# One transfer per unit for the time steps of a state-space scan

## The chip, the cores and the metric

The kernel runs on one core of a Trainium2 chip. The metric is the device time of one execution in microseconds (us). Of three timed executions of the kernel before the change the median is 6779.58 us (6778.02 to 6794.15). A separate execution was recorded by the hardware profiler; the profile below is of that one.

## The reference, cut to what matters

Four layers work on a batch of four images of 32 x 32 positions (1024 tokens) with 256 channels: a convolution with a state-space scan (layer 0), a bottleneck convolution (layer 1), masked attention with a mixture of experts (layer 2), and a second state-space scan with a mixture of experts (layer 3). The change touches the two scans alone. Both have 512 inner channels; the first has N = 64 states for each channel, the second N = 16. In layer 0, with `xt`, `dtt`, `Bt` and `Ct` of one token:

```python
dt = softplus(dt_raw @ w_dt + dt_bias)        # [batch, token, 512]
A = -exp(A_log)                               # [512, N]
def step(h, inp):
    xt, dtt, Bt, Ct = inp
    dA = exp(dtt[:, :, None] * A)
    h = dA * h + (dtt * xt)[:, :, None] * Bt[:, None, :]
    y = einsum('bdn,bn->bd', h, Ct)
    return (h, y)
```

Layer 3 does the same with its own `dt`, `A`, `B`, `C` and N = 16. What matters below: `dt` has one value for each channel and token, and every state of a channel needs that same value, multiplied by its own entry of `A`.

## The kernel before

**Units of a scan.** A scan of one image is cut into units. One unit fills the 128 partitions with the (channel, state) pairs of G = 128 / N channels: partition g * N + s holds state s of the unit's channel g. So G is 2 in layer 0 and 8 in layer 3. The free dimension holds the 1024 tokens. Scan (0, b) is that of layer 0 for image b and has 256 units; scan (3, b) is that of layer 3 and has 64. They run in the order `SCANS` of line 31: (0,0), (0,1), (3,0), (0,2), (3,1), (0,3), (3,2), (3,3); 1280 units in all, of which 1024 have G = 2 and 256 have G = 8.

**What one unit does** (`scans`, line 351). The steps of unit k are:

- `load` (line 416): G DMAs, issued by SyncE (SP in the profile). Each reads one row of 1024 floats (4 KB) of `dt` from DRAM and writes it to the N partitions of its channel, into its part of the tile `dA` (128 x 1024 floats, 512 KB). The tile has five buffers.
- `decay` (line 431): ScalarE turns the tile in place into exp(A * dt); A comes as a scale for each partition.
- `first` (line 441): two TensorE matmuls spread dt * x over the states into the PSUM tile `ps_rep`.
- in the loop (line 497): VectorE multiplies `ps_rep` by the tile of B (`rows`).
- line 503: VectorE runs the recurrence with `tensor_tensor_scan` from `dA` and `ps_rep` into `h`; line 504: GpSimd multiplies `h` by the tile of C.
- `pair` (line 456): for every two units TensorE sums over the states into `ps_y`; at the end of a group ScalarE copies the result to `yo`, and SP stores it.

**Order.** The order of every engine's instructions is fixed when the program is built. At step k the loop first calls `load(k + 4)`, then `first(k + 1)`, then `decay(k + 2)`; the VectorE work of unit k follows. As `dA` has five buffers, the load of unit k + 4 waits until the scan of unit k - 1 has read the last tenant of its buffer. SP issues all loads and stores of the kernel from one queue, in order: when it waits for a buffer, everything behind it waits too. Each DMA also waits for the one issued eight before it, since eight semaphores are used in turn.

**What runs between the units.** The other layers are generators (`front`, `middle`, `last`, line 33) that yield a piece of work at a time. `run` (line 548) puts up to two pieces between the steps of the scan, by estimated costs of instructions (`Metered`, line 92) kept in a clock for each engine; the estimates do not count DMAs issued by SP. So TensorE, ScalarE, VectorE and GpSimd alternate between scan units and pieces of other layers, and SP between loads of `dA` and the other layers' loads and stores, such as expert weights (`we`, lines 1452 and 1454), the scan results read back (`y_back`, line 782) and the stores of `dt` and its split product (lines 614 and 629). Before the first scan, `load_vectors` (line 191), `weight` (line 227), `rows` (line 221) and the `prepare` functions load small vectors and matrices; the vectors of `VEC_PACKS` (line 51) come with one DMA for each name, of 1 to 36 rows of 512 bytes, and `w2s` (line 859) with one of 4 rows of 9 pieces.

All compute instructions issued in the interleaved part carry line 124 in the profile, that of the wrapper that meters them. The loads of `dA` carry line 425.

Of the kernel before, what the change touches and what calls it, by code (L numbers as in the profile page):

```python
# [18 lines left out]
L = 1024  # L19
# [113 lines left out]
class Hybrid:  # L133
# [217 lines left out]
    def scans(self, mp, psum):  # L351
# [7 lines left out]
        nc = self.nc  # L359
        units = []  # L360
        for scan in SCANS:
            G = P // self.states[scan[0]]
# [53 lines left out]
        def load(k):  # L416
            if k >= len(units):
                return
            scan, d, c, i, j = units[k]
            n = self.states[scan[0]]  # L420
            G = P // n
            a = mp.tile([P, L], F32, tag="dA", name="dA", bufs=5)
            for g in range(G):
                r = 64 * c + 32 * j + G * i + g
                nc.sync.dma_start(  # L425
                    a[g * n : (g + 1) * n, :],
                    self.mem["dt", *scan, d][r : r + 1, :].to_broadcast([n, L]),
                )
            state[k] = a

        def decay(k):
# [53 lines left out]
        for k in range(4):  # L485
            load(k)
# [3 lines left out]
        for k in range(len(units) + 4):  # L490
            waits = chunks_ahead(k)
            load(k + 4)
            if not waits:
                first(k + 1)
            decay(k + 2)
            if k < len(units):
                a, inp = state.pop(k)
                B, Cm = rows[units[k][0]]
                nc.vector.tensor_tensor(inp, inp, B, ALU.mult)
            yield  # L500
            if k < len(units):
                h = mp.tile([P, L], F32, tag="h", name="h", bufs=5)
                nc.vector.tensor_tensor_scan(h, a, inp, 0.0, ALU.mult, ALU.add)
                nc.gpsimd.tensor_tensor(h, h, Cm, ALU.mult)
                state[k] = h
            if k % 2 == 1 and 2 <= k < len(units) + 2:
                pair(k - 2)
            if waits:
                chunks_ahead(k, True)
                first(k + 1)  # L510
            yield
# [1332 lines left out]
```

## Time and profile before

| what | value |
|---|---|
| timed executions | 6779.58 us median of 3 (6778.02 to 6794.15) |
| the profiled execution's own time | 6786.48 us |
| its span, first to last instruction | 6784.8 us |
| busy: TensorE, VectorE, GpSimd, ScalarE | 79%, 77%, 54%, 51% of the span |
| granted TensorE clock | 0.827 of full speed |
| DMA traffic | 937.44 MB, mean 138 GB/s |
| hardware DMA queue | 391696 packets, 930.53 MB, 52.1% of 16 engines' span |
| first and last scan instruction start | 207.4 us and 6343.7 us |
| SP waiting for VectorE's `h` before a load of `dA` | 2405.8 us in 871 waits |
| ScalarE waiting for a load of `dA` | 990.5 us in 366 waits |

The span counts from the first to the last instruction of the profiled execution; its own time lies 1.7 us above it. Busy shares are means over stages with different limits, so they do not tell what bounds a stage. An engine's wait is idle time of that engine before an instruction, put down to whatever released it last; idle time of an engine that does not bound a stage costs nothing. A DMA packet is one piece that one of the core's 16 DMA engines moves; the share of the queue is the time that packets took, over all 16. The table by stretches of time, used below, gives the busy time of each engine in a stretch, then the granted TensorE clock, the mean busy share of the 16 DMA engines and what they moved.

### The profile page before, as it was taken

What the parts mean: (1) busy time and instruction counts of PE and PEld (TensorE: products, weight loads), DVE (VectorE), ACT (ScalarE), POOL (GpSimd) and SP (SyncE); (2) the same over time, 40 slices, a digit from 0 to 9 for tenths busy, and PEclk for the clock granted to TensorE, in tenths of its full rate; (3) what the DMA queues carried; (4) which work ended last, traced back from release to release, by engine and by line L of the source; (5) the groups of instructions that cost most, each with busy time, mean ns of one, the idle gap of its engine ahead of it and who ended that gap; (6) DMA issues with size and microseconds to landing.
All of it is one profiled execution on the core that took longest, in us unless ns stands there. A gap on an engine that the chain in (4) does not pass through costs nothing. (4 is left out here: it accounts for less than half of the span.)

```text
span 6784.8 us, 65796 instructions
## 1 busy us (share of the span) xinstructions
PE 5361.8 (79%) x20236; PEld 2166.3 (32%) x20320; DVE 5227.3 (77%) x4486; ACT 3447.1 (51%) x4112; POOL 3649.0 (54%) x1801
## 2 busy tenths in 40 slices
PE   6558778679798568979689679898698688967979
PEld 3002213122252022234145232253254222514556
DVE  8778998978798997789889987898899871247411
ACT  2426666445477334557558445476386344245411
POOL 0876786755457665555856655556756551054200
PEclk8559778589798578979789789898699788977989
DMA  2556665754365765446656755456666750146221
GB/s 73 147 144 160 179 171 155 193 133 124 102 164 158 185 162 143 116 117 178 180 148 170 184 149 132 107 140 176 177 167 171 167 133 14 50 130 151 79 62 35
DMA packets 394235, 937.44 MB, mean 138 GB/s; under 512 B 83220, under 2 KB 165728, under 8 KB 392224
## 3 DMA queue, kind: packets, MB, share of 16 engines
q1 hardware_dynamic: 391696, 930.53, 52.1%
q8 instruction: 172, 2.82, 0.2%
q0 software_dynamic: 2128, 2.13, 0.2%
q14 instruction: 239, 1.96, 0.1%
HBM read 842.59 MB, written 93.95 MB: 138 GB/s over the span
## 5 line engine op out<-in xcount | busy, mean ns | idle before, releaser
L124 POOL TENSOR_TENSOR h<-h,rows 128x1024 f32<-128x1024 f32 x1280 | 3031.3, 2371 | 1999.9 <-DVE h L124 1649.9
L124 DVE TENSOR_TENSOR_SCAN h<-dA,ps_rep 128x1024 f32<-128x1024 f32 x1280 | 2925.2, 2285 | 234.0 <-issue 106.0
L124 DVE TENSOR_TENSOR ps_rep<-ps_rep,rows 128x1024 f32<-128x1024 f32 x1280 | 1552.8, 1213 | 287.8 <-PE ps_rep L124 287.3
L124 ACT ACTIVATE dA<-dA,A_L_conv_A_log 128x1024 f32<-128x1024 f32 x1024 | 1154.2, 1145 | 727.6 <-DMA dA<-dt 636.5
L124 PE MATMUL ps_rep<-S,spread_L_conv_A_log 96*128 96x512 bf16 x2048 | 766.7, 465 | 740.7 <-DVE h L124 709.1
L124 PE MATMUL ps_y<-h,collect_L_conv_A_log 128*32 128x512 f32 x4096 | 804.1, 762 | 96.0 <-POOL h L124 94.6
L124 PE MATMUL ps_h<-xTm,we 128*128 128x512 f32 x1536 | 719.4, 608 | 3.4 <-ACT h_m L124 1.8
L124 PE MATMUL ps_e<-we,h_m 128*128 128x256 f32 x3072 | 703.2, 382 | 10.9 <-ACT h_m L124 10.4
L124 ACT ACT_TABLE_LOAD x495 | 635.1, 1283 | 76.2 <-PE ps_h L124 44.4
L124 PEld LDWEIGHTS <-spread_L_conv_A_log 96*128 96x128 bf16 x2048 | 161.6, 103 | 1520.5 <-DVE h L124 1209.6
L124 PEld LDWEIGHTS ps_e<-we,h_m 128*128 128x128 f32 x3072 | 583.3, 191 | 157.2 <-issue 45.4
L124 DVE SCALAR_TENSOR_TENSOR tb<-ps_e,cw,tb 128x256 f32<-128x256 f32 x512 | 220.7, 474 | 415.5 <-PE ps_e L124 415.5
L124 ACT ACTIVATE h_m<-ps_h,cols 128x512 f32<-128x512 f32 x384 | 260.4, 686 | 473.8 <-PE ps_h L124 471.0
L124 ACT ACTIVATE dA<-dA,A_L_attn_A_log 128x1024 f32<-128x1024 f32 x256 | 293.5, 1148 | 390.3 <-DMA dA<-dt 354.0
L124 ACT ACTIVATE p<-ps_sc 128x512 f32<-128x512 f32 x432 | 234.4, 594 | 450.6 <-PE ps_sc L124 295.5
L124 PEld LDWEIGHTS ps_h<-xTm,we 128*128 128x128 f32 x1536 | 292.9, 194 | 341.8 <-issue 295.2
L124 PE MATMUL ps_at<-p,v 128*32 128x512 f32 x1024 | 357.6, 616 | 45.8 <-ACT p L124 35.1
L124 PE MATMUL ps_rep<-S,spread_L_attn_A_log 96*128 96x512 bf16 x512 | 185.4, 451 | 205.8 <-DVE h L124 184.3
L124 PE MATMUL ps_sc<-qT,kT 32*128 32x512 f32 x864 | 251.7, 654 | 42.1 <-ACTq L1248 24.5
L124 PE MATMUL ps_at<-p,ones 128*32 128x512 f32 x1024 | 275.1, 616 | 0.0
L124 PEld LDWEIGHTS ps_y<-h,collect_L_conv_A_log 128*32 128x32 f32 x4096 | 107.9, 120 | 495.9 <-POOL h L124 248.3
L124 PE MATMUL ps_cv<-pad,diag 128*128 128x512 f32 x576 | 260.4, 594 | 0.0
(311 smaller groups left out, 5012.4 us busy)
## 6 DMA issues: line engine op xcount, KB each, us to landing
dA<-dt SPq DMA_DIRECT2D x2048, 256.0 KB
dA<-dt SPq DMA_DIRECT2D x2048, 64.0 KB
we<-in_L_ffn_W_dram SPq DMA_DIRECT2D x64, 512.0 KB
parts<-parts SPq DMA_DIRECT2D x64, 384.0 KB
S<-parts SPq DMA_DIRECT2D x96, 256.0 KB
dt<-sp_r SPq DMA_DIRECT2D x64, 256.0 KB
y<-yo SPq DMA_DIRECT2D x128, 128.0 KB
y_back<-y SPq DMA_DIRECT2D x64, 256.0 KB
```

Of the source, the lines that this page charges most:

```text
L124: return got(*args, **kw)
```

## The change

Instead of one DMA for each channel of a unit, `load` issues one DMA for the unit. Its source is a view of G rows of `dt` with a repeated dimension in between: G rows, each taken n times (step 0), each of 1024 floats. Its destination is the whole tile of 128 partitions. The bytes moved into the tile are the same, 512 KB; the pieces of 4 KB are the same 128.

```diff
             a = mp.tile([P, L], F32, tag="dA", name="dA", bufs=5)
-            for g in range(G):
-                r = 64 * c + 32 * j + G * i + g
-                nc.sync.dma_start(
-                    a[g * n : (g + 1) * n, :],
-                    self.mem["dt", *scan, d][r : r + 1, :].to_broadcast([n, L]),
-                )
+            r = 64 * c + 32 * j + G * i
+            nc.sync.dma_start(
+                a,
+                self.mem["dt", *scan, d][r : r + G, :].unsqueeze(1).to_broadcast([G, n, L]),
+            )
             state[k] = a
```

In the built program the source of such a load has the dimensions 2 x 64 x 1024 (layer 0) or 8 x 16 x 1024 (layer 3), the destination 128 x 1 x 1024. Before, source and destination were 64 x 1024 or 16 x 1024 both. SP issues 1280 loads of `dA` in place of 4096 (2048 with N = 64 and 2048 with N = 16). The order of the instructions on TensorE, VectorE, ScalarE and GpSimd is unchanged, and so is the place of each unit's load among SP's other DMAs.

## The prediction

> **What bounds the kernel now.** I read the page's table of groups first, then the table by stretches of time, cut where the scans change, then SP's issues and the waits, and at last the DMA view of the first 26 us, where transfers of few rows stand. The chain of work that ended last is no help here: its engine shares add up to some 8% of the span and its long pieces lie in the tail after 6353 us.
>
> From the page:
>
> ```profile
> span 6784.8 us, 65796 instructions
> ...
> L124 DVE TENSOR_TENSOR_SCAN h<-dA,ps_rep 128x1024 f32<-128x1024 f32 x1280 | 2925.2, 2285 | 234.0 <-issue 106.0
> L124 DVE TENSOR_TENSOR ps_rep<-ps_rep,rows 128x1024 f32<-128x1024 f32 x1280 | 1552.8, 1213 | 287.8 <-PE ps_rep L124 287.3
> ```
>
> One unit costs VectorE 2.285 + 1.213 = 3.50 us, and the 1280 units 4478 of its 5227.3 busy us. Now all engines in the four long stretches, one for each scan of layer 0 (256 units each; the same view kept to `dA` counts 256 or 257 scan instructions in each):
>
> ```profile
> core 0: us, PE busy (x) PEld busy (x) DVE busy (x) ACT busy (x) POOL busy (x), PEclk, DMA share, GB/s
> 207.40:1277.50 1070.10, 767.51 (x2251) 198.08 (x2250) 946.15 (x633) 587.74 (x739) 811.56 (x435) 0.72 0.62 164
> 1277.50:2435.00 1157.50, 887.14 (x3519) 304.28 (x3541) 999.77 (x769) 582.22 (x689) 692.73 (x326) 0.80 0.56 148
> ...
> 2739.50:3874.10 1134.60, 946.01 (x3744) 405.97 (x3749) 1008.12 (x813) 707.54 (x769) 683.55 (x320) 0.86 0.59 156
> ...
> 4179.20:5314.70 1135.50, 946.26 (x3744) 406.43 (x3749) 1007.82 (x814) 707.68 (x769) 683.24 (x320) 0.86 0.59 156
> ```
>
> VectorE is busy 3961.9 of their 4497.7 us (88%); it bounds them. A unit takes 4497.7 / 1024 = 4.39 us. The 16 DMA engines are busy 56 to 62%, so they are no bound, but with less than a factor of two to spare. That spare is what this change has to be held against.
>
> SP's issues of the loads, from the view of tile `dA` (shortest, median and longest ns), and what VectorE waits for, over the whole span:
>
> ```profile
> L425 SPq DMA_DIRECT2D dA<-dt x4096: 302/444/5038, 197.2 to 6333.3; - x196
> ```
>
> ```profile
> DVE h L124 <- DMA dA<-dt: 51.1, 135, 7.7
> ```
>
> The loads cost VectorE itself only 51.1 us. ScalarE's 990.5 us of waiting for them is slack of an engine busy half the time.
>
> **What decides: over how many DMA engines one transfer is spread.** The start of the program has DMAs of few rows. The DMA view of 0 to 14 us and of 14 to 26 us (GB/s in 40 slices; packets):
>
> ```profile
> GB/s 0 0 0 0 0 82 143 29 149 266 360 377 392 366 363 386 421 410 407 291 113 21 0 0 6 4 3 1 1 3 1 1 1 1 3 4 3 12 6 6
> DMA packets 1480, 1.62 MB, mean 116 GB/s; under 512 B 104, under 2 KB 1224, under 8 KB 1480
> ```
>
> ```profile
> DMA packets 2473, 1.82 MB, mean 152 GB/s; under 512 B 508, under 2 KB 2472, under 8 KB 2472
> ```
>
> No data packet of the first window is under 512 B, so the 104 small ones are something else: one for each engine that a transfer uses. Test it: the transfers there have 128 rows (two), 36 (one), 8 (one), 4 (eight), 2 (five) and 1 (ten). If each takes the largest number up to 16 that divides its rows, that gives 2 x 16 + 12 + 8 + 8 x 4 + 5 x 2 + 10 = 104, exactly; 16 for each would be 432. In the second window a matrix of 32-byte rows gives 256 small data packets, leaving 252. The transfers with 16, 32, 64, 128 or 8 rows give 248; `w2s` (4 rows of 9 pieces each) must give the other 4. Its 36 pieces went over 4 engines, not 12: the outermost dimension decides.
>
> The new load's source has outermost dimension 2 (8 in layer 3), its destination 128. No transfer of before has two sides that differ, so the trace does not show which counts. Bounds: 2 engines (the source's) and 16 (the destination's). I take 2: each engine needs a whole share of both sides, and `w2s` is the nearest row, as its pieces were not used to spread it wider.
>
> [...]
>
> **The price of a piece.** A load of a layer 0 unit is 128 pieces of 4096 B, on two engines 64 each. Lower end: the best slice above moved 421 GB/s over 16 engines, 26.3 GB/s each, so 4096 B take 155.7 ns. Upper end: in the stretch from 207 us, 164 GB/s at 0.62 busy is 164 / (16 x 0.62) = 16.5 GB/s for a busy engine, 248 ns. There most packets come from sixteen engines reading the same 4 KB row at once; with two engines on two different rows that crowd is gone. I take 155.7 ns: 64 x 0.1557 = 9.96 us for a unit, against 4.39 us now. [...]
>
> **The sum, against the profiled span.**
>
> - Outside the four stretches: 6784.8 - 4497.7 = 2287 us, left as it is (layer 3's part below).
> - Loads of 1024 units: 65,536 pieces x 155.7 ns = 10,204 us, end to end on the same two engines.
> - Other traffic of those stretches on these two: 164 x 1070.1 + 148 x 1157.5 + 156 x 1134.6 + 156 x 1135.5 us = 701 MB, less 1024 x 0.524 = 537 MB of `dA`, leaves 164 MB, 10.25 MB for each engine: 390 us at 26.3 GB/s, 621 at 16.5. I take 500.
> - Gaps in which the two engines run empty. Four loads stand ahead of use, 40 us of queue, so SP's issue, ScalarE's exp (1.15 us) and the scan (2.29 us) lie beneath it. But another layer's load now queues behind up to four of ours; where an engine needs it at once, the scan stops, the queue drains, and it must start again: exp 1.15, scan 2.29, issue 0.44 and about 1 us until bytes move (in the GB/s line above the first slice with bytes begins at 1.75 us, and SP issued that DMA at 0.80), some 5 us. Between none and 300 places (a good third of SP's roughly 800 other DMAs) this is 0 to 1500 us. I take 350, some 70 places, as expert weights and `S` are asked for long ahead.
>
> Sum: 2287 + 10,204 + 500 + 350 = 13,341 us of span, with 1.7 us around it 13,343. The median of the timed runs is 7 us (0.1%) below the profiled one, which is nothing here: 13,340.
>
> **What is taken away counts little.** SP issues 1280 loads, not 4096. A new issue is not shown: between 0.302 us (the shortest now) and 0.588 us (the median of the stores of `yo`, L479); either is nothing beside 10 us. The wait removed is covered by the transfer that is now late: ScalarE waits for `dA`, VectorE for ScalarE, and behind VectorE's scan stand its pieces of other layers, then GpSimd and TensorE, and at last SP's next load, which needs the buffer.
>
> **Layer 3's 256 units** go over 8 engines: 16 pieces each, 2.5 us (4.0 at 248 ns), under the 4.76 us that a unit takes in 2435.0 to 2739.5 us. Cost 0 to +50 us; a gain is bounded by VectorE's idle time in the three plain stretches, 57.5 + 58.2 + 69.3 = 185 us. I take zero: VectorE waited 13.1 us for `dA` in the first of them.
>
> **Rivals.**
>
> - **Sixteen engines after all** (not slower): the destination's 128 partitions set the spread. Then a load takes at most 2 us, SP saves half or more of its issues, and what can go is VectorE's 51.1 us and a little of its idle time: 6,745 us, between 6,650 and 6,790. For it: the same bytes, pieces and partitions. Against it: `w2s`. The point from which this decides is 128 x 0.1557 us / engines + 0.4 us of other traffic < 4.39 us, that is 5 engines or more.
> - **Two engines at the crowded price** of 248 ns: 65,536 x 0.248 = 16,253; with 2287 + 621 + 350 it is 19,510 us. For it: it is the mean now. Against it: the cause of the crowd goes.
> - **One engine**, if the two sides cannot be matched: 20,407 + 2287 + 850, about 23,500 us. Only single-row transfers did this.
>
> **Chances and range.** Two engines near the full rate: 0.82. Two engines, crowded: 0.09. Sixteen or another number from five up: 0.07. One engine: 0.02. The forecast's own range goes from 12,800 (390 us of other traffic, no gaps, a little less outside) to 15,000 (all gaps, or a piece of 170 ns with part of them); it holds nearly all of the first case, and leaves out the others, 0.18 together. About 0.3% is what a measurement of this kernel can tell from no change. Faster by more than that 0.04, within it 0.03, slower 0.93.
>
> **What would show it.** The four layer 0 stretches take about 2.7 ms each; ScalarE's idle time before `dA` goes to several ms, released by the load of `dA`; the DMA share in these stretches falls to about 2 of 16 engines plus the rest, 0.15 to 0.2, and GB/s to 55 to 70; VectorE's busy time in all stays at 5227 us; SP shows 1280 issues; small packets fall by 61,440, as a unit's loads end on 2 or 8 engines in place of 2 x 16 or 8 x 16. Layer 3's stretches stay near 305 us. It would be wrong if the DMA share rose or the layer 0 stretches stayed near 1100 us.

## The result, and the profile after

| | before | after |
|---|---|---|
| timed executions | 6778.80 us median of 4 (6777.09 to 6794.15) | 13278.42 us median of 4 (13268.95 to 13293.59) |
| ratio, 95% interval | 1 | 1.958 [1.9545, 1.9616] |
| the profiled execution's own time, its span | 6786.48, 6784.8 us | 13293.59, 13291.9 us |
| layer 0's four stretches together | 4497.7 us | 10,914.2 us |
| layer 3's four stretches together | 1642.1 us | 1725.3 us |
| rest of the span | 645.0 us | 652.4 us |

The kernel takes nearly twice as long. Of the 6507 us that were added to the span, 6417 lie in layer 0's stretches, 83 in layer 3's and 7 elsewhere. Layer 3's last stretch ends with the last unit's work on VectorE, 3.5 us after the last scan starts. From the page of the kernel after, the span, all DMA packets, and the groups of the scan and of the exp before it (busy us, mean ns; then idle us before it and what ended most of that):

```profile
span 13291.9 us, 60144 instructions
...
DMA packets 332752, 936.84 MB, mean 70 GB/s; under 512 B 21780, under 2 KB 104288, under 8 KB 330784
...
L124 DVE TENSOR_TENSOR_SCAN h<-dA,ps_rep 128x1024 f32<-128x1024 f32 x1280 | 2924.8, 2285 | 3440.5 <-ACT dA L124 3270.8
...
L124 ACT ACTIVATE dA<-dA,A_L_conv_A_log 128x1024 f32<-128x1024 f32 x1024 | 1175.1, 1148 | 6635.0 <-DMA dA<-dt 6507.1
```

The work itself is the same: a scan still takes 2285 ns. What is new is the idle time before it, 3440.5 us in place of 234.0, put down to ScalarE's exp, which in turn waited for the load. The small packets fell from 83,220 to 21,780; before, the line of the DMA packets was

```profile
DMA packets 394235, 937.44 MB, mean 138 GB/s; under 512 B 83220, under 2 KB 165728, under 8 KB 392224
```

Now the stretches, as in the table before (layer 0, layer 0, layer 3, layer 0, layer 3, layer 0):

```profile
core 0: us, PE busy (x) PEld busy (x) DVE busy (x) ACT busy (x) POOL busy (x), PEclk, DMA share, GB/s
215.10:2920.20 2705.10, 889.89 (x2250) 232.75 (x2250) 923.91 (x633) 593.73 (x736) 801.22 (x435) 0.58 0.17 64
2920.20:5642.40 2722.20, 1087.96 (x3541) 349.55 (x3541) 991.17 (x769) 587.37 (x689) 685.56 (x326) 0.63 0.17 64
5642.40:5981.30 338.90, 250.82 (x1069) 89.14 (x1069) 248.85 (x195) 135.62 (x178) 168.88 (x79) 0.82 0.53 128
5981.30:8724.00 2742.70, 1220.98 (x3762) 489.05 (x3760) 1000.80 (x813) 711.39 (x767) 677.76 (x320) 0.66 0.18 65
8724.00:9059.70 335.70, 253.07 (x1067) 90.17 (x1067) 247.49 (x195) 135.02 (x177) 168.79 (x79) 0.82 0.52 130
9059.70:11803.90 2744.20, 1227.18 (x3762) 493.43 (x3762) 1002.19 (x814) 712.11 (x769) 677.83 (x320) 0.65 0.18 65
```

No engine is busy for half of a layer 0 stretch, and the DMA engines together are busy for 17 to 18%. Nothing looks loaded, because a mean over 16 engines hides two that hardly rest: 0.17 x 16 is 2.7 engines' worth, two of it for `dA`. In the packet records of the first stretch exactly two pieces of 4 KB are under way for 2440 of its 2705 us. The timeline of VectorE in a plain part of the second stretch (start us, us, then the instruction, and in brackets the idle time before it) shows the beat:

```profile
3377.39 2.29 DVE L124 TENSOR_TENSOR_SCAN h<-dA,ps_rep 128x1024 f32<-128x1024 f32 x1 [12.39 <-ACT dA L124]
3379.60 1.21 DVE L124 TENSOR_TENSOR ps_rep<-ps_rep,rows 128x1024 f32<-128x1024 f32 x1
3387.49 2.29 DVE L124 TENSOR_TENSOR_SCAN h<-dA,ps_rep 128x1024 f32<-128x1024 f32 x1 [6.69 <-ACT dA L124]
3389.70 1.21 DVE L124 TENSOR_TENSOR ps_rep<-ps_rep,rows 128x1024 f32<-128x1024 f32 x1
3397.58 2.29 DVE L124 TENSOR_TENSOR_SCAN h<-dA,ps_rep 128x1024 f32<-128x1024 f32 x1 [6.67 <-ACT dA L124]
```

A unit every 10.1 us: 3.4 us of work and 6.7 us of waiting. SP's queue shows the same beat from the other side. SP's timeline at the first units (start us, us of the run of issues):

```profile
197.22 33.35 SPq L424 DMA_DIRECT2D dA<-dt  x5
230.68 9.81 SPq L628 DMA_DIRECT2D parts<-parts  x1
240.58 4.17 SPq L613 DMA_DIRECT2D dt<-sp_r  x1
244.84 17.50 SPq L424 DMA_DIRECT2D dA<-dt  x3
```

Two loads are issued at once (0.6 and 0.5 us), the third issue holds SP for 12.3 us, and from then on each takes 9.8 to 9.9 us, with no buffer missing. We read this as full queues behind SP, in which room comes free only as the two engines move pieces. The store of `parts`, which has nothing to do with `dA`, waits in the same way. In a plain part (3362 to 3403 us) SP's issues follow one another every 9.94 us, which is 64 pieces at 155 ns.

### The profile page after: what moved, and what is told of

It reads as the page before. It is cut to its first block, busy times and chain, and to the rows that moved or that the text cites. A ratio compares the mean times of both kernels' runs of the same rounds, so it can differ in the third digit from the quotient of the medians.

```text
span 13291.9 us, 60144 instructions
## 1 busy us (share of the span) xinstructions
PE 6276.6 (47%) x20320; PEld 2421.3 (18%) x20320; DVE 5186.0 (39%) x4486; ACT 3471.3 (26%) x4112; POOL 3617.0 (27%) x1801
## 2 busy tenths in 40 slices
DMA packets 332752, 936.84 MB, mean 70 GB/s; under 512 B 21780, under 2 KB 104288, under 8 KB 330784
## 5 line engine op out<-in xcount | busy, mean ns | idle before, releaser
L124 DVE TENSOR_TENSOR_SCAN h<-dA,ps_rep 128x1024 f32<-128x1024 f32 x1280 | 2924.8, 2285 | 3440.5 <-ACT dA L124 3270.8
L124 PE MATMUL ps_rep<-S,spread_L_conv_A_log 96*128 96x512 bf16 x2048 | 874.7, 522 | 3553.1 <-DVE h L124 3503.3
L124 PE MATMUL ps_h<-xTm,we 128*128 128x512 f32 x1536 | 910.8, 740 | 766.5 <-ACT h_m L124 578.7
L124 PE MATMUL ps_e<-we,h_m 128*128 128x256 f32 x3072 | 828.2, 429 | 384.3 <-ACT h_m L124 384.1
L124 PEld LDWEIGHTS ps_e<-we,h_m 128*128 128x128 f32 x3072 | 659.4, 218 | 591.1 <-ACT h_m L124 446.9
L124 PE MATMUL ps_at<-p,v 128*32 128x512 f32 x1024 | 455.6, 806 | 495.2 <-ACT p L124 491.1
L124 PEld LDWEIGHTS ps_h<-xTm,we 128*128 128x128 f32 x1536 | 346.7, 235 | 1225.8 <-ACT h_m L124 634.8
L124 PE MATMUL ps_cv<-pad,diag 128*128 128x512 f32 x576 | 338.4, 740 | 159.1 <-ACT diag L124 159.1
L124 POOL TENSOR_TENSOR sp_l<-sp_l,sp_e 128x512 f32<-128x512 f32 x64 | 81.0, 1265 | 1066.5 <-ACT parts L124 768.9
L124 PE MATMUL ps_at<-p,ones 128*32 128x512 f32 x1024 | 369.1, 809 | 0.0
L124 PE MATMUL ps_sc<-qT,kT 32*128 32x512 f32 x864 | 314.8, 808 | 59.2 <-ACTq L1247 59.2
```

Of the source, the lines that this page charges most:

```text
L124: return got(*args, **kw)
```

## The experiments

The theory: a transfer is spread over as many engines as divide the outermost dimensions of both its sides, so layer 0's loads run on 2 engines, and the rate of those two sets the time. The rivals: the form with a repeated dimension is itself slow; or the price of a piece, not the number of engines, makes the loss. Each layer's part, the number of engines, the price of a piece and the number of transfers are taken apart below. Where stretches are given, they are cut at the first scan instruction of each scan, as before. Prices of a piece are means over the packet records of 4 KB in the stretch named.

**Each layer alone (e2, e3).** The changed load for one layer, the loop over channels for the other:

```diff
+            if n == 64:        # e2; e3 has n == 16
                 r = 64 * c + 32 * j + G * i
                 nc.sync.dma_start(a, ...unsqueeze(1).to_broadcast([G, n, L]))
+            else:
+                for g in range(G):
...
```

> The change in layer 0 alone; layer 3 has its eight transfers for each unit again. Engine theory: all of the lost time belongs to layer 0, so 13,180 to 13,280 us (at most the 90 us that the layer 3 stretches and the rest grew by comes back). If layer 3 carried a real part, the time would fall by several hundred us.

Measured: 13,236.53 us (13,236.20 to 13,236.85), ratio 1.9523 [1.9488, 1.9559]. All but a little of the loss is layer 0's, as expected.

> The change in layer 3 alone, on eight engines: 16 pieces, 2.5 us a unit; layer 0 has its two transfers again. Engine theory: within 6,730 to 6,840 us of time, as 2.5 to 4.0 us lies under the 4.76 us that such a unit takes before. Issue theory, if the form and not the engines held SP for 9 us: 256 x (9.2 - 4.8) = 1,130 us more, about 7,900 us.

Measured: 6855.54 us (6849.60 to 6864.34), ratio 1.0115 [1.0099, 1.0131]: 76 us slower, above what was expected. Layer 3's first two stretches take 328 us in place of 305, with 8 of 16 engines used: the same loads in the kernel after had exactly eight pieces of 4 KB under way for 194 of the 339 us of layer 3's first stretch (16 of 305 before). The first of them before, then two of e3:

```profile
2435.00:2739.50 304.50, 238.70 (x1068) 86.64 (x1080) 247.01 (x195) 133.98 (x177) 169.85 (x79) 0.87 0.59 147
```

```profile
2424.50:2752.50 328.00, 243.07 (x1068) 88.93 (x1080) 247.01 (x195) 135.11 (x178) 168.88 (x79) 0.83 0.57 137
3888.60:4216.50 327.90, 245.65 (x1068) 90.03 (x1080) 246.94 (x195) 135.13 (x178) 168.85 (x79) 0.83 0.56 137
```

A share of 0.57 again hides which engines it is. A 4 KB packet took 261 ns in the first of these stretches, so the 8192 pieces of its 64 loads keep each of 8 engines busy for 8192 x 0.261 / 8 = 267 us; all other packets, taken as spread evenly over 16 engines, add 52 us: 320 of 328 us. By this estimate these 8 engines are full.

**Sixteen engines with one transfer (e1).** The same one transfer for a unit, with the repeat outermost. Partition s * G + g then holds state s of channel g; the tables that depend on this order (A, `spread`, `collect`, the tiles of B and C) are built in it; the tiles of B and C come with 16 transfers in place of 80. All kernels below in this order (e6, e8, e9, e10) share that.

```diff
                 a,
-                self.mem["dt", *scan, d][r : r + G, :].unsqueeze(1).to_broadcast([G, n, L]),
+                self.mem["dt", *scan, d][r : r + G, :].unsqueeze(0).to_broadcast([n, G, L]),
```

> One load per unit as in the change, but with the partitions in the order (state, channel), so that the source's outermost dimension is the repeat: 64 x 2 x 1024 in layer 0, 16 x 8 x 1024 in layer 3. The tables of A, the spreading and collecting matrices and the rows of B and C are permuted to fit; the result is the same. Engine theory (the slower time comes from two engines moving 64 pieces each): 16 engines with 8 pieces each, a layer 0 unit back at 4.3 to 4.5 us, 6,650 to 6,850 us in all, SP's issues mostly under 1 us. Rival, issue theory (the issue of a source with a repeated inner dimension itself holds SP for about 9 us, as the median of 9.16 us in the changed kernel reads at first sight): still one issue of such a form per unit, so about 13,300 us. Rival, lateness (one large transfer lands later than two halves, five buffers are too few): between the two, well above 7,000 us.

Measured: **6640.68 us** (6639.17 to 6652.76), ratio 0.980 [0.9787, 0.9814]. It is 2% faster than the kernel before. So one transfer with a repeated dimension is not slow in itself; the place of the repeat decides. Its first stretches (layer 0, layer 0, layer 3):

```profile
203.90:1256.30 1052.40, 771.77 (x2252) 197.13 (x2250) 955.24 (x633) 585.33 (x738) 812.95 (x435) 0.71 0.52 167
1256.30:2396.00 1139.70, 873.50 (x3519) 300.28 (x3541) 996.06 (x770) 581.83 (x690) 694.80 (x326) 0.81 0.46 150
2396.00:2686.40 290.40, 234.69 (x1067) 85.62 (x1080) 246.15 (x195) 132.37 (x177) 169.88 (x79) 0.89 0.61 154
```

Against before, the DMA share of the first stretch fell from 0.62 to 0.52 with as many bytes, the layer 0 stretches together from 4497.7 to 4434.9 us, and layer 3's from 1642.1 to 1561.4. That is more than the rival of sixteen engines had allowed; the runs from e7 on look for the reason.

**Four and eight engines (e4, e5).** `dt` of layer 0 is stored two or four times, so that the source has 4 x 32 x 1024 or 8 x 16 x 1024 dimensions (the extra stores are 8 or 25 MB). Layer 3's load is the changed one.

```diff
+            q = 2 if n == 64 else 1        # e5: 4
+            nc.sync.dma_start(
+                a,
+                self.mem["dt", *scan, d][r : r + G].rearrange("g q t -> (g q) t")
+                .unsqueeze(1).to_broadcast([G * q, n // q, L]),
+            )
```

> The change, with each row of layer 0's dt stored twice in DRAM, so that a unit's source is 4 x 32 x 1024; still one load per unit with the same 128 pieces. Engine theory: four engines, 32 pieces of 155 ns = 4.97 us, with the other traffic and gaps of about 0.7 us 5.5 to 5.8 us a unit: 1024 x 5.7 + 2,350 = about 8,150 us (7,800 to 8,500). Issue theory: still about 13,300 us.

> The change, with each row of layer 0's dt stored four times in DRAM, so that a layer 0 source is 8 x 16 x 1024 as in layer 3: eight engines, 16 pieces each, 2.5 us a unit. By the criterion of the prediction (nothing lost from five engines up): at most the 6,856 us of the run with layer 3 alone changed. By what layer 3 showed on eight engines (0.3 us a unit more, although 2.5 us lies under the unit's time): 6,856 + 1024 x 0.3 = about 7,160 us.

Measured: four engines 8257.25 us (8253.11 to 8261.39), ratio 1.2179 [1.2157, 1.2201], as expected; eight engines 7220.99 us (7198.08 to 7236.84), ratio 1.0644 [1.0623, 1.0664], which is nearest to the second of the two sums: "nothing lost from five engines up" is wrong.

| engines of a layer 0 load | kernel | ns of a 4 KB packet, layer 0 | layer 0's stretches, us | time, us |
|---|---|---|---|---|
| 2 | after | 163 to 170 | 10,914 | 13,278 |
| 4 | e4 | 164 to 174 | 5895 | 8257 |
| 8 | e5 | 231 to 240 | 4848 | 7221 |
| 16 | e1 | 197 to 200 | 4435 | 6641 |

From 2 to 4 engines the stretches shrink by nearly half, as they must if the rate of the engines used sets the time. At eight the price of a piece jumps. In the second stretch of e5 (1204.7 us) 32,768 pieces at 240 ns on 8 engines are 984 us, the other packets, taken as spread evenly, 150 us on each engine: 1134 of 1204.7 us, 94% full. The extra stores are not the reason: their pieces have 2 KB, and layer 0's second to fourth stretches hold as many 2 KB packets as before, yet take 47 to 75 us more than before. With four or eight engines the form with one DMA costs little to issue. SP's issues and ScalarE's waits in the view of tile `dA`, first of e4:

```profile
L425 SPq DMA_DIRECT2D dA<-dt x1280: 500/574/9282, 200.5 to 7792.9; - x183
...
  DMA dA<-dt: 2786.8, 724
```

then of e5:

```profile
L425 SPq DMA_DIRECT2D dA<-dt x1280: 567/575/4664, 196.8 to 6774.1; - x183
...
  DMA dA<-dt: 1685.8, 531
```

The median issue is 574 and 575 ns, against 9164 with two engines.

**Different rows at the same time (e7).** The kernel before, but each transfer reads n different rows of `dt` in place of one row n times (always the same 128 rows). The units so get the `dt` of wrong channels; number, size and place of the pieces are unchanged.

```diff
-                r = 64 * c + 32 * j + G * i + g
+                r = 64 * g if n == 64 else 16 * g
...
-                    self.mem["dt", *scan, d][r : r + 1, :].to_broadcast([n, L]),
+                    self.mem["dt", *scan, d][r : r + n, :],
```

> The kernel before, each of its transfers reading 64 (or 16) different rows of dt where it read one row 64 (or 16) times; dt is so taken from wrong channels, and the output is not the reference's. Bytes, pieces, engines, issues and waits are unchanged. If the long pieces of the kernel before (mean 244 ns) come from sixteen engines reading one row at once: pieces near 160 ns, the DMA share in the layer 0 stretches from 0.56 to 0.62 down to about 0.4. The time would then tell what the crowd costs: nothing (6,780 us) if the loads are hidden, 50 to 100 us less if late loads are part of VectorE's idle time.

Measured: 6776.06 us (6767.66 to 6781.93), ratio 0.9996 [0.9987, 1.0005]. The first stretch, beside 0.62 and 164 GB/s before:

```profile
204.80:1271.20 1066.40, 765.81 (x2251) 197.21 (x2250) 942.47 (x633) 587.58 (x739) 811.85 (x435) 0.72 0.61 165
```

In layer 0's stretches a 4 KB packet takes 243 to 251 ns, against 247 to 249 before. That many engines read the same row does not make layer 0's price. In layer 3's stretches, all but the third, it does have a part: 222 to 225 ns in place of 257 to 265, but all of layer 3's stretches gain only 6 us by it.

**Two transfers for a unit, cut two ways (e6, e8).** Both in the order of e1. e6 cuts a unit into two halves of 64 neighbouring partitions, e8 into two halves of 512 columns over all 128 partitions:

```diff
+            for g in range(2):                                   # e6
+                nc.sync.dma_start(
+                    a[64 * g : 64 * g + 64, :],
+                    ...[r : r + G, :].unsqueeze(0).to_broadcast([n // 2, G, L]),
+                )
...
+            for g in range(2):                                   # e8
+                cols = slice(512 * g, 512 * g + 512)
+                nc.sync.dma_start(
+                    a[:, cols],
+                    ...[r : r + G, cols].unsqueeze(0).to_broadcast([n, G, 512]),
+                )
```

> The state-major order with two transfers for each unit again, one for each half of the partitions, each over 16 engines with 4 pieces. Same order, same rows read by each engine; only issues and semaphores per unit go from one to two. Theory A (the 140 us that the state-major kernel gained over the kernel before come mainly from VectorE's scan and ScalarE's exp waiting for one DMA semaphore in place of two, 0.06 us a unit: units of 3.54 us in place of 3.60): the 3.60 us come back, about 6,700 to 6,740 us. Theory B (the gain is from how the engines share the rows, mean 210 ns in place of 244 ns for a piece of 4 KB): the gain stays, 6,630 to 6,660 us.

> The state-major order with two transfers for each unit again, but cut along the tokens: each writes all 128 partitions, 512 of the 1024 columns, over 16 engines with 8 pieces of 2 KB. Issues and semaphores are as with the halves of the partitions; only the partitions that one transfer reaches differ. Semaphore theory alone (what the halves lost against one transfer, 209 us, is the second wait): about 6,850 us, as with the halves. [...]

Measured: halves 6849.63 us (6828.87 to 6861.12), ratio 1.0105 [1.0088, 1.0122], which neither theory had; columns 6663.92 us (6660.40 to 6668.09), ratio 0.9828 [0.9815, 0.9842], 186 us below the 6,850 of the semaphore theory: the second wait alone is not what the halves lost. But the two are not a clean pair in layer 3: with halves, the source there is 8 x 8 x 1024, and the number of small packets, 53,524 against 57,620 for the columns, is smaller by 512 x 8, as it must be if each of these 512 halves ran on 8 engines. A layer 3 stretch of the halves, then of the columns:

```profile
2416.80:2749.40 332.60, 245.14 (x1070) 89.56 (x1082) 247.29 (x196) 134.72 (x178) 168.63 (x79) 0.83 0.56 135
```

```profile
2406.60:2700.80 294.20, 240.26 (x1068) 88.20 (x1080) 246.54 (x196) 131.96 (x177) 169.50 (x79) 0.87 0.56 152
```

The halves' 332.6 us look like e3's 328.0, which also had 8 engines. The next run keeps halves for layer 0 alone.

**Halves in layer 0, whole transfers in layer 3 (e10).**

```diff
+            cuts = 2 if n == 64 else 1
+            m = P // cuts
+            for g in range(cuts):
+                nc.sync.dma_start(
+                    a[m * g : m * g + m, :],
+                    ...[r : r + G, :].unsqueeze(0).to_broadcast([n // cuts, G, L]),
+                )
```

> State-major order, layer 0's units by two transfers of 64 neighbouring partitions each (32 x 2 x 1024, 16 engines), layer 3's by one transfer (16 x 8 x 1024, 16 engines). In the earlier run with halves in both layers, a half of a unit of layer 3 had a source of 8 x 8 x 1024, and so only 8 engines. Theory A, those 8 engines made layer 3's loss: layer 3's stretches as with whole transfers, 1,561 us, layer 0's as with halves, 4,482: 6,690 us (6,670 to 6,710). Theory B, halves cost layer 3's stretches time by what they do to the queue as a whole: 6,720 us and more.

Measured: 6690.75 us (6679.63 to 6692.95), ratio 0.9872 [0.9856, 0.9887]: theory A. Layer 3's stretches are back at 1558.5 us, so e6's loss there was the 8 engines. Layer 0's four stretches are 4486.2 us with a 4 KB packet at 245 to 249 ns. Within this one kernel the shortest usual distance of two scans is 3.60 us where a unit has two transfers and 3.54 us where it has one. The same two distances in layer 0, first in the kernel before (two transfers), then in e1 (one):

```profile
527.08 2.29 DVE L124 TENSOR_TENSOR_SCAN h<-dA,ps_rep 128x1024 f32<-128x1024 f32 x1 [0.19 <-issue]
...
530.68 2.29 DVE L124 TENSOR_TENSOR_SCAN h<-dA,ps_rep 128x1024 f32<-128x1024 f32 x1 [0.19 <-issue]
```

```profile
534.77 2.29 DVE L124 TENSOR_TENSOR_SCAN h<-dA,ps_rep 128x1024 f32<-128x1024 f32 x1
...
538.31 2.29 DVE L124 TENSOR_TENSOR_SCAN h<-dA,ps_rep 128x1024 f32<-128x1024 f32 x1
```

**One transfer for each channel, over the whole range of partitions (e9).** The order of e1, but again 4096 transfers, each of one row to n partitions that lie G apart:

```diff
+            parts = a.rearrange("(n g) t -> g n t", g=G)
+            for g in range(G):
+                nc.sync.dma_start(
+                    parts[g],
+                    self.mem["dt", *scan, d][r + g : r + g + 1, :].to_broadcast([n, L]),
+                )
```

> Partitions ordered (state, channel), and one transfer for each channel again (2 or 8 for a unit, 4096 in all), each of one row of dt to n partitions that lie 2 or 8 apart over the whole range of 128: number of transfers, pieces of 4 KB and engines (16) as in the kernel before, only the place of the partitions differs. Theory A, the range of partitions that a transfer reaches sets the price: layer 0's stretches add up to some 4,460 us as with two transfers of half the columns, layer 3's to some 1,570, together 6,665 us (6,640 to 6,700). Theory B, the number of transfers and of waits sets it: as before, 4,498 and 1,642, 6,780 us (6,760 to 6,800). A mix, layer 0 by A and layer 3 by B: 6,740.

Measured: 6962.15 us (6958.48 to 6970.01), ratio 1.0277 [1.0263, 1.0291], which neither theory gives. The stretches show why: theory A is right in layer 0, and neither is in layer 3. Layer 0's are 4459.3 us, as theory A has it, with a 4 KB packet at 184 to 188 ns. Layer 3's are 1865.9 us, worse than before. The first stretch of each:

```profile
202.60:1256.30 1053.70, 767.46 (x2252) 195.77 (x2250) 958.03 (x633) 585.48 (x738) 813.08 (x435) 0.71 0.49 166
2407.90:2772.20 364.30, 250.56 (x1079) 89.94 (x1082) 247.66 (x196) 135.54 (x178) 168.87 (x79) 0.81 0.42 125
```

Nothing in the second line is full, the DMA engines (0.42) least of all, and a 4 KB packet is cheaper there than before (209 against 257 ns). What is full is SP's time. SP's timeline in layer 3's first stretch, 64 loads of `dA` in a row: the kernel before, then e9.

```profile
2642.43 30.91 SPq L425 DMA_DIRECT2D dA<-dt  x64
```

```profile
2660.62 41.03 SPq L432 DMA_DIRECT2D dA<-dt  x64
```

64 issues are 8 units: 3.9 us of SP for a unit before, 5.1 us in e9, whose issues of strided partitions take a median of 587 ns in this stretch, against 418 (shortest, median and longest ns, before and e9):

```profile
L425 SPq DMA_DIRECT2D dA<-dt x488: 302/418/2586, 2435.0 to 2738.4; - x163
```

```profile
L432 SPq DMA_DIRECT2D dA<-dt x497: 451/587/2927, 2407.9 to 2771.1; - x166
```

Over this stretch all of SP's waits add up to 39.8 of 304.5 us in the kernel before, 20.4 of 364.3 us in e9 and 220.0 of 290.4 us in e1; for the rest SP was issuing, 87%, 94% and 24% of the time (the short pauses between two issues counted in). The largest part of the waits in e1, SP's waits for VectorE's `h` before a load, in the kernel before and in e1 (us in total, times, longest):

```profile
SPq L425 <- DVE h L124: 16.5, 16, 3.9
```

```profile
SPq L430 <- DVE h L124: 167.5, 51, 8.1
```

An SP that is ahead waits for buffers, as in e1. Before, it hardly did: in layer 3 it was behind most of the time. In e9 each issue got longer, and the stretch with it, by 60 us, though the pieces got cheaper. So SP's eight issues for a unit held up layer 3, and that is what one transfer takes away: 81 us in e1 and, with two transfers, 75 us in e8 (1567.2 us), while a 4 KB packet in layer 3 costs e1 254 to 261 ns, nearly as before (257 to 265).

A rival for these 81 us is the number of DMA semaphores for which VectorE's queue waits at each unit of layer 3: eight before, two in e8, none in e1. The distances of the scans there speak against it. The shortest usual one is 3.60 us with eight waits and with two, 3.54 us with none, and some 100 of 252 distances are of this kind: 100 x 0.06 = 6 us, which is what e8 gains less than e1.

What made layer 0 faster in e1 is another thing. By layer 0's stretches:

| layer 0's load, 16 engines | kernel | 4 KB packet, ns | four stretches, us |
|---|---|---|---|
| two transfers, each to 64 neighbouring partitions | before, e10 | 247 to 249, 245 to 249 | 4497.7, 4486.2 |
| two transfers, each to 64 partitions, every second | e9 | 184 to 188 | 4459.3 |
| two transfers of half the columns, 128 partitions | e8 | (2 KB: 97 to 99) | 4458.3 |
| one transfer to 128 partitions | e1 | 197 to 200 | 4434.9 |

Two transfers cost 23 or 24 us more than one. With that the same, a transfer that reaches the whole range of partitions saves another 27 to 39 us, and its pieces are a fifth to a quarter cheaper. The stretches are those of one profiled execution for each kernel; the timed runs of e10 and e8 bear them out, 6690.75 and 6663.92 us, 27 us apart with no overlap of their runs.

## Why the prediction was right, and where its steps were not

13,340 us were predicted, 13,278 measured, and the step that carried the sum, the number of engines, is shown by the series of 2, 4, 8 and 16.

- **Two engines, by the source's outermost dimension.** Right. The small packets fell by 83,220 - 21,780 = 61,440, as forecast to the packet. The same count also fits the other runs exactly: e4 has 1024 x 2 more for its loads and 32 x 16 for its extra stores (24,340), e5 1024 x 6 and 96 x 16 (29,460), e1 1280 x 16 in place of 4096 for its loads and 64 x 16 fewer for the tiles of B and C (37,140). With 2, 4, 8 and 64 as the source's outermost dimension and 128 as the destination's, a layer 0 load so ran on 2, 4, 8 and 16 engines, and a layer 3 load with 8 or 16 on 8 or 16. The reason given, that each engine needs a whole share of both sides, was an estimate; these counts agree with it. Two halves of the partitions in layer 0 are 50 us slower than one transfer if the repeat stands outermost (e10 6691 us, e1 6641); against one transfer with the repeat inside, the halves of the kernel before are 6500 us faster (6779 us, 13,278 after).
- **155.7 ns for a piece on these two.** Right: 9.94 us for 64, 155 ns. 1024 such units are 10,179 us; the rest of the stretches, 735 us, stands against 850 taken for other traffic and gaps.
- **Why a piece costs 248 ns before** ("sixteen engines reading the same 4 KB row at once"). The step failed, though the value taken did not: e7 has different rows and the same price in layer 0. In its place the runs show, for layer 0, the range of partitions: 247 to 249 ns for 64 neighbours (before), 197 to 200 for all 128 (e1), 184 to 188 for 64 spread over 128 (e9). That is a fifth to a quarter off the price of a piece, with 27 to 39 us off the time; by what means the range does it, no run shows. Layer 3's runs do not agree: e1's transfers reach all 128 partitions there too, and a piece costs nearly what it did (254 to 261 ns against 257 to 265), while different rows (e7) do make it cheaper (222 to 225). What sets the price in layer 3 stays open.
- **"5 engines or more" as the point where the loss ends.** Failed. Two terms were too small at eight engines: the price of a piece (155.7 ns taken, 231 to 240 measured) and other traffic (0.4 us a unit taken, 150 us / 256 = 0.6 us measured). 16 x 0.24 + 0.6 = 4.4 us is the unit's own mean of 4.39 us, so these engines were full on average. Our reading, not tried by itself, is that they are then late whenever units come faster, as they do between other layers' pieces (every 3.54 us).
- **Layer 3: "Cost 0 to +50 us", zero taken.** Failed, by the same two terms: 83 us, 77 of which e3 shows with layer 3 changed alone. The sign that it named, stretches near 305 us, failed too (339 and 336 us). The sum compared 2.5 us (4.0 at the high price) with 4.76 us and left the other traffic out; measured are 267 us / 64 = 4.2 us, and 0.8 us of other traffic, 5.0 us, against the 5.1 us that a unit took in e3 (328 us / 64). The true price lay at the high end of the bounds and a little above (261 ns).
- **SP's issues "either is nothing".** Failed twice. In layer 3 SP was issuing for 87% of the stretch before and held the units up; the issues that the change saves are worth 75 to 81 us. The prediction had a row that showed part of this and took zero all the same: the 13.1 us that VectorE waited for `dA` in the first of layer 3's stretches are nearly what e1 gains there (304.5 to 290.4 us). Half of the gain lies in the last stretch (315.8 to 275.4 us), where VectorE's wait for `dA` was only 10.6 us; SP's own queue would have shown it, as SP waited for 52.7 us of that stretch and was issuing in the rest. And the new issue was not 0.30 to 0.59 us but 9.2 us in the median. No more time was lost by that than the sum had, as the two engines were the bound; the form itself costs 0.51 to 0.58 us, as e1, e4 and e5 show.
- **"Four loads stand ahead of use, 40 us of queue."** Failed in size: SP was held from the third load on. When a unit's exp starts, two later loads are issued and a third is being issued in 346 of the first 512 units. Gaps stayed small all the same: times of over 0.5 us in which no 4 KB piece moved add up to some 95 us in the four stretches.
- **The rival of sixteen engines at 6,745 (6,650 to 6,790).** The case did not come, but e1 is what it describes, and gave 6,641, just below its range. Its price took 51.1 us of VectorE's waits and a little of its idle time. The runs showed 81 us in layer 3, by SP's queue, and 63 us in layer 0, by the range of partitions and the second transfer.

So the gain that one transfer offers is real, some 80 us in layer 3, and it went into new waits: 8 engines took back more than that in layer 3, and 2 engines cost eighty times as much in layer 0. The fastest of all these kernels is e1.

## What to carry to other kernels

As far as these runs tell, a transfer with a repeated dimension should have its outermost dimension divisible by 16 on both sides: with 2, 4, 8 and 64 as the source's in layer 0 the kernels took 13,278, 8257, 7221 and 6641 us. If the layout of the destination is free, put the repeat outermost and the few rows inside, as e1 does. Before merging transfers, count the engines each one will run on, and compare pieces for each engine, at the price of a crowded stretch (here 231 to 261 ns on 8 engines, against 155 on 2) and with all other traffic on it, with the unit's fastest rate (3.54 us), not its mean (4.39 us). And read the issuing queue's own time by stretches: an engine that only issues does not appear as busy, yet it held up layer 3, where SP was issuing for 87% of the first stretch.

## What the runs showed of the hardware that was not expected

- With two engines behind on 64 pieces for each load, SP's issues themselves took 9.8 us, also for a DMA with another target (the store of `parts`, 9.79 us in the median against 0.54 before). We read it as a full queue that holds the engine that issues; the trace shows only the long issues.
- A piece costs 155 ns when 2 engines carry the loads, 164 to 174 as a packet mean with 4, 231 to 240 with 8, 247 with 16 on 64 neighbouring partitions and 184 to 200 with 16 on the whole range, all in layer 0. Why eight engines pay nearly as much as sixteen on half the range stays open; it was not tried by itself.
- Issuing a DMA to 16 partitions, every eighth, takes longer than to 16 neighbours: a median of 587 ns against 418 (e9 and before, layer 3). It is not the stride alone: with 64 partitions, every second or neighbours, the median is 582 ns in both (layer 0, 300 to 700 us).
- A second transfer for a tile costs VectorE time even where nothing is late: in e10 units follow at 3.60 us with two and 3.54 us with one. In the traces VectorE's queue waits for the semaphores of two DMAs at most units of layer 0 in the kernel before, and for none in e1, but eight waits (layer 3, before) cost no more than two. In layer 0 some 470 to 490 of 1020 distances are of this shortest kind in all these kernels: 470 x 0.06 = 28 us, near the 23 or 24 us above. That the semaphores are the cause is not shown apart from this.
